# Encoder, window attention, encoder as one stream of 40 attention jobs, with the feed-forward inside the attention's steps

## The chip, the cores and the metric

The kernel runs on one core of a Trainium2 chip. A core has five engines that work at the same time, each through its own queue and in order: PE (matrix products), DVE (vector operations), ACT (activations and copies with a scale and a bias), POOL (GpSimd, here for selects, small vector work and gathers through lists of indices) and SP (which only starts transfers). They wait for each other by semaphores. PE's weight loads, PEld in the profile, overlap its products. PE writes to PSUM, eight banks of 128 partitions x 512 numbers. The metric is the time on the device in microseconds, the median of several runs.

## The reference

A network of 16 layers works on `x`, 8 batches of T = 256 tokens of D = 128 numbers (in some layers cut otherwise), each with a layer norm ahead and the result added to `x`. The change concerns the last three: a mixture of encoder layers, a banded attention, the same mixture again. Cut to these:

```python
x = x + L3_ffn(layernorm(x))          # encoder mixture
x = x + L3_attn_b(layernorm(x))       # banded attention, 16 heads of 8, window 64
x = x + L3_ffn(layernorm(x))          # encoder mixture again

def L3_ffn(x):                        # E = 4 experts, K = 2 are chosen per batch
    gate = x.mean(axis=1) @ gate_w.T + gate_b
    weights = softmax(gate) * (the two largest, per batch)
    return sum over experts of weights * encoder_layer(x, the expert's matrices)

def encoder_layer(x, ...):
    q, k, v = split(x @ iw.T + ib)                 # 16 heads of 8
    o = softmax(q @ k.T / sqrt(8)) @ v
    x = layernorm(x + o @ ow.T + ob) * n1w + n1b
    ff = relu(x @ l1w.T + l1b) @ l2w.T + l2b       # 128 -> 512 -> 128
    return layernorm(x + ff) * n2w + n2b
```

The kernel handles 8 batches of 256 tokens, so one encoder mixture is 8 x 2 = 16 jobs, each one batch through one expert.

## The kernel before

`Net.stages` lists the parts of the network, which run one after another. The last three are `encoder_moe` (L1999), `window` (which calls `attn8`, L1511) and `encoder_moe` again.

**An encoder stage.** First the layer norm of all 8 batches (`layernorm`, L1224): statistics of 16 tiles on DVE, a root on ACT and a reciprocal on DVE (`rstd_of`, L1189), then per batch the normalized rows `xn` and their transpose `xnT` over PE. Then the gate: mean over the tokens (`g_mean`), a product on PE (`g_ps`), and a chain of small DVE operations that finds the two experts of each batch, their weights (`g_wt`) and the rows at which the experts' matrices lie in HBM (`g_idx`). From here on each job's weights come by indirect gathers that POOL issues (L2076): `g_A` (774 numbers per partition, the matrices of q, k, v and the output projection), `g_RA` (256, biases), `g_B` (1024, the feed-forward's matrices) and `g_RC` (263, its biases and scales).

**The attention** of the 16 jobs is a pipeline over steps (`StripAttention`, run under a manual schedule: PE's order is the order of the code, while the other engines' orders are found by the scheduler of the framework). A job has four steps, one per group of four heads. In step s a *burst* (L117 to L150) computes the scores `ps_s` of group s (reduced by DVE to the negative row maxima `nsp`, L154) and, for group s-2, the scores once more, transposed and with the maximum subtracted, `ps_t`, of which ACT takes the exponential into `pt`. The maximum gets into the product through `ps_m` and `qa` (L183, L185). Behind the burst a step does what is entered for it: the product with the values `ps_o` for the group of step s-3 (`av`), then the parts of neighbouring jobs: q, k and v projections at -4, -2 and +1 steps from a job's start, the transposes and the division of the result (`half`, `ps_ot`), and two steps of `finish`: the transpose `ps_tr`, and the output projection `ps_r`, which DVE adds to `xr` (input and bias) and writes to `zt`. In this stage all eight PSUM banks are one ring, `sml`, of which each new product takes the next.

**The feed-forward** (`ExpertFeed`, L700) comes after the attention of all 16 jobs. Per job: `norm` (ACT writes `gxh`), `turn` (transposes `g_t`, ACT writes `gy` and `gyr` with the norm's scale and bias), `up` (`g_h`, two products of 2 x 256 columns; ACT and DVE write the rectified `g_hs`), `down` (`g_f`: identity times `gyr` plus four products, for each half of the tokens), then statistics, root, and the addition of the second norm's result to `x` (L790 to L805). The weights `g_B` of the first four jobs are gathered into `g_ring` during the attention's end; the other twelve go to tiles of their own (`g_late`), fetched as the feed-forward starts. PSUM is divided otherwise here: four banks `sml`, two for `g_t`, two for `g_f`.

**The window stage** (`attn8` with kind "w") is the same pipeline with 8 jobs, a band mask added to the scores, and selects on POOL that clear the weights outside the band (`keep01`, L1325). Its layer norm has statistics ahead for all batches, and rows and transposes per job inside the steps. Then the second encoder stage starts with its layer norm and its gate for all batches.

Of the kernel before, what the change touches and what calls it, by code (L numbers as in the profile page):

```python
# [40 lines left out]
class Job:  # L41
    def __init__(self, xT, w_q, w_k, w_v, b_q, b_k, b_v, finish):
        self.xT, self.w_q, self.w_k, self.w_v = xT, w_q, w_k, w_v
        self.b_q, self.b_k, self.b_v, self.finish = b_q, b_k, b_v, finish


class StripAttention:
# [19 lines left out]
    def __init__(self, net, wk, opens, scale, kind, ln):  # L67
        self.net, self.nc, self.wk, self.opens, self.ln = net, net.nc, wk, opens, ln
        self.scale, self.kind = scale, kind
        self.sb, self.tb = self.S_BLOCKS[kind], self.T_BLOCKS[kind]  # L70
        self.width = {None: 512, "c": 384, "w": 320}[kind]
        self.jobs = {}
# [30 lines left out]
    def burst(self, s, last):  # L103
        net, nc = self.net, self.nc
        halves = ((0, 1), (2, 3))
        tops, sums = {}, {}
        if 0 <= s < last:
            tops = {g: net.sml("ps_s") for g in (range(4) if self.kind else ())}
            for ps in tops.values():
                nc.tensor.matmul(  # L110
                    out=ps[:, : self.width], lhsT=net.identb,
                    rhs=net.masks[self.kind][:, : self.width], start=True, stop=False,
                )
        t = s - self.LAG
        if 0 <= t < last:
            jt, it = self.jobs[t // 4], t % 4
            jt.pts[it] = self.wk.tile(  # L117
                [P, 4, self.width], F32, tag="pt", name="pt", bufs=2 if self.kind is None else 4
            )
        for sub in range(2):  # L120
            calls, then = [[], []], []
            if 0 <= s < last:
                j, i = self.jobs[s // 4], s % 4
                for g in halves[sub]:
                    then.append(self.score(j, s // 4 % 2, i, g, tops.get(g), calls))
            if 0 <= t < last:
                for g in halves[1 - sub]:
                    then.append(self.weigh(jt, it, g, calls))
            for cs in calls:
                for c in cs:  # L130
                    nc.tensor.matmul(**c)  # L131
            for f in then:
                f()
        if 0 <= t < last and self.kind is not None:
            net.keep01(jt.pts[it], self.kind)

    def score(self, j, n, i, g, ps, calls):
# [4 lines left out]
        for c, (qt, k0, nk, c0) in enumerate(self.sb):  # L142
# [3 lines left out]
                    rhs=j.kT[r, i // 3, k0 : k0 + nk], start=self.kind is None,  # L146
                    stop=self.kind is None or c == 1,
# [4 lines left out]
        def top():  # L152
            if self.kind is None:
# [3 lines left out]
            else:  # L157
                for qt, k0, nk, c0 in self.sb:
# [6 lines left out]
    def weigh(self, j, i, g, calls):  # L165
# [3 lines left out]
        for c, (kt, q0, nq, c0) in enumerate(self.tb):  # L169
# [6 lines left out]
        out = j.pts[i][:, g, :]  # L176
        return lambda: nc.scalar.activation(out, ps[:, : self.width], AF.Exp, scale=self.scale)  # L177
# [10 lines left out]
    def av(self, n, i):  # L188
# [4 lines left out]
        net.av8(po, j.pts[i], j.va, 4 * i, self.O_BLOCKS[self.kind])  # L193
        nc.scalar.copy(j.oT[:, i, :], po[:, :T])  # L194

    def half(self, n, qt):
        net, j = self.net, self.jobs[n]
        if qt == 0:
            j.o = self.wk.tile([P, 2, D], F32, tag="o8", name="o8")
            j.end = j.finish(self.wk, j.o)  # L200
        net.normal8_half(self.wk, j.o, j.oT, qt)

    def open(self, n):
        j = self.jobs[n] = self.opens[n]()
        j.qa, j.pts = {}, {}

    def finish(self, n):
        f = next(self.jobs[n].end, None)
        if f:
            f()  # L210

    def run(self):
        ev = {}

        def at(s, order, f, *args):
            ev.setdefault(s, []).append((order, f, args))

        N = len(self.opens)
        av = self.AV[self.kind]
        for n in range(N):  # L220
            b = 4 * n
            for i in range(4):
                at(b + i, 9, self.lower, n, i)
                at(b + i + av, 1, self.av, n, i)
            at(b - 6, 0, self.open, n)
            if self.ln:
                at(b - 6, 0, self.net.ln_norm, n)
                at(b - 5, 5, self.net.ln_turn, n)
            for d, f in zip(self.QKV[self.kind], (self.q, self.k, self.v)):
                at(b + d, 3, f, n)  # L230
            e = b + av + 4
            at(e, 6, self.half, n, 0)
            at(e, 6, self.half, n, 1)
            at(e + 1, 4, self.finish, n)
            at(e + 2, 2, self.finish, n)
        for s in range(min(ev), max(ev) + 1):
            self.burst(s, 4 * N)
            for order, f, args in sorted(ev.get(s, ()), key=lambda e: e[0]):
                f(*args)
# [460 lines left out]

class ExpertFeed:
    JOBS = 2 * B

    def __init__(self, net, wk, zt, mv, wf, gather):
        self.net, self.nc, self.wk, self.zt, self.mv, self.wf = net, net.nc, wk, zt, mv, wf
        self.gather_rows = gather
        self.ring = net.w16.tile([P, 4, 1024], F32, tag="w16", name="g_ring")
        self.hs = net.w16.tile([P, 4, 4, T], F32, tag="w16", name="g_hs")
# [5 lines left out]
    def fetch(self, i):  # L714
        w = self.ring[:, i, :] if i < 4 else self.late.tile(
# [1680 lines left out]
```

## Time and profile before

| | us |
|---|---|
| median of 3 runs | 2954.19 (2953.16 to 2958.8) |
| the profiled execution | 2984.23 |
| its span, first to last instruction | 2982.5 |

| place in the span | us from its start |
|---|---|
| first encoder: attention's first step | 2011.6 |
| its last burst; first `g_h` of the feed-forward | 2305.9; 2320 |
| window stage in its steady steps | about 2437 to 2544 |
| second encoder: first step | 2582.6 |
| last `g_f` | 2977 |

The page of a profile lists, for each engine, busy time, its share and the number of instructions; then the span in 40 slices, a digit for the busy tenths of each (PEclk is the granted clock of PE in tenths); then groups of instructions by line and tile. A table of stretches gives, for each stretch of the span, its length and the busy time (and number of instructions) of PE, PEld, DVE, ACT and POOL, the mean clock, the mean busy share of the DMA engines and the GB/s that they moved. A row for a tile gives the least, median and longest duration in ns of each operation on it.

### The profile page before, as it was taken

Reading aid. Unit: us, or ns where it says so; the run is one execution under the profiler, and the core shown is the slowest. Engines: PE = TensorE matmul, PEld = TensorE weight load, DVE = VectorE, ACT = ScalarE, POOL = GpSimd, SP = SyncE. Lnnn points to the kernel's source line nnn. Section 1 sums busy time; section 2 is a strip of 40 time slices with the busy share of each in tenths; the row PEclk is TensorE's granted clock in tenths of the full one; section 3 lists DMA queues with packets and bytes.
Section 4 is the critical chain, followed back from the end, with each engine's and each line's share of the span. In section 5 each row is a group of like instructions: output and inputs, shape, how many; then the busy total and the mean of one; then the engine's idle time right before and its main releaser. Section 6 shows DMA issues by size and latency. Waiting matters only on the chain. (4 is left out here: it accounts for less than half of the span.)

```text
span 2982.5 us, 63419 instructions
## 1 busy us (share of the span) xinstructions
PE 2567.0 (86%) x25520; PEld 1823.8 (61%) x25520; DVE 1979.9 (66%) x5033; ACT 1466.6 (49%) x3385; POOL 1092.8 (37%) x1404
## 2 busy tenths in 40 slices
PE   5888779989599978875996699978999889699998
PEld 2444358866377756753665476645666667466667
DVE  3888856667566666545763677756777577577756
ACT  3666424455244433312651455535666545366654
POOL 3777559612398124122002444431110336311121
PEclk8999989999799989977998899988999899799999
DMA  3000000000000100012001200011110300111112
GB/s 101 0 1 1 31 29 1 1 2 2 2 1 1 57 1 2 1 54 20 2 19 46 11 1 1 1 29 54 32 30 13 107 2 3 39 53 30 29 61 68
DMA packets 41988, 70.03 MB, mean 23 GB/s; under 512 B 9048, under 2 KB 30560, under 8 KB 40928
## 3 DMA queue, kind: packets, MB, share of 16 engines
q0 software_dynamic: 12288, 42.17, 5.7%
q1 hardware_dynamic: 29408, 23.81, 2.7%
q8 instruction: 202, 3.31, 0.5%
q14 instruction: 90, 0.74, 0.1%
HBM read 58.88 MB, written 7.08 MB: 22 GB/s over the span
## 5 line engine op out<-in xcount | busy, mean ns | idle before, releaser
L177 ACT ACTIVATE pt<-ps_t 128x512 f32<-128x512 f32 (+2 forms) x896 | 430.9, 566 | 303.9 <-PE ps_t L131 294.7
L154 DVE TENSOR_REDUCE nsp<-ps_s 128x2 f32<-128x512 f32 x640 | 399.3, 684 | 96.4 <-PE ps_t L131 62.1
L131 PE MATMUL ps_t<-qa,k 32*128 32x256 f32 (+2 forms) x3584 | 443.3, 377 | 7.0 <-DVE qa L185 3.5
L131 PE MATMUL ps_s<-k,q 32*128 32x256 f32 (+2 forms) x3584 | 427.8, 380 | 5.8 <-ACT k L95 5.1
L131 PEld LDWEIGHTS ps_t<-qa,k 32*128 32x128 f32 x3584 | 327.8, 187 | 28.4 <-ACT q L83 10.9
L131 PEld LDWEIGHTS ps_s<-k,q 32*128 32x128 f32 x3584 | 296.1, 189 | 59.1 <-issue 35.6
L1290 PE MATMUL ps_o<-pt,vaug 128*32 128x256 f32 (+3 forms) x3840 | 226.3, 354 | 15.5 <-DVE nsp L154 3.7
L1330 POOL TENSOR_SCALAR_AFFINE_SELECT pt<-pt 128x768 f32<-128x768 f32 (+1 forms) x192 | 129.3, 705 | 224.8 <-ACT pt L177 176.4
L464 POOL TENSOR_TENSOR hw<-hw,hden 128x512 f32<-128x512 f32 x128 | 130.3, 1039 | 175.9 <-DVE hden L461 99.0
L984 POOL TENSOR_TENSOR h<-h,cs 128x512 f32<-128x512 f32 x128 | 166.1, 1317 | 61.3 <-DVE h L983 58.7
L1290 PEld LDWEIGHTS ps_o<-pt,vaug 128*32 128x32 f32 x3840 | 101.7, 109 | 115.1 <-DVE nsp L154 54.2
L159 DVE TENSOR_REDUCE nsp<-ps_s 128x1 f32<-128x128 f32 (+2 forms) x512 | 132.4, 330 | 54.7 <-PE ps_t L131 47.4
L558 POOL TENSOR_SCALAR oh<-iota,f_tr 128x128 f32<-128x128 f32 (+1 forms) x256 | 139.1, 552 | 78.5 <-PE f_xg L569 43.3
L2076 POOL DMA_INDIRECT g_A<-in_g_A,g_idx x32 | 30.4, 948 | 368.7 <-ACT oT L194 229.3
L1219 PE MATMUL ln_ps<-ident,xn 128*128 128x128 f32 x256 | 62.8, 352 | 112.9 <-DVE xn L1211 108.6
L185 DVE TENSOR_TENSOR qa<-q,ps_m 128x256 f32<-128x256 f32 x224 | 93.1, 415 | 91.8 <-PE ps_m L183 62.0
L995 PE MATMUL m_py<-h,ident 128*128 128x512 f32 x256 | 137.5, 645 | 18.2 <-POOL h L984 16.5
L983 DVE TENSOR_TENSOR_SCAN h<-m_da,db 128x512 f32<-128x512 f32 x128 | 150.2, 1206 | 3.4 <-POOL m_ug L901 1.4
L1219 PEld LDWEIGHTS ln_ps<-ident,xn 128*128 128x128 f32 x256 | 37.4, 162 | 140.6 <-issue 83.8
L183 PE MATMUL ps_m<-ident,nsp 128*128 128x128 f32 x448 | 96.5, 294 | 26.4 <-DVE nsp L154 18.8
L457 ACT ACTIVATE hw<-h_s,hm 128x256 f32<-128x256 f32 x256 | 117.3, 476 | 1.4 <-DVE hm L451 1.3
L977 ACT ACTIVATE m_da<-delta,m_a 128x510 f32<-128x510 f32 x128 | 87.3, 689 | 55.2 <-DVE h L983 52.9
(490 smaller groups left out, 6088.3 us busy)
## 6 DMA issues: line engine op xcount, KB each, us to landing
mw<-in_e_w SPq DMA_DIRECT2D x2, 2048.0 KB, 8.2
moe_x<-e_bx SPq DMA_DIRECT2D x4, 640.0 KB, 5.5
e_bx<-moe_x SPq DMA_DIRECT2D x4, 640.0 KB, 5.4
x<-in_x SPq DMA_DIRECT2D x4, 256.0 KB, 3.7
fraw<-in_f_wq SPq DMA_DIRECT2D x1, 1024.0 KB
fraw<-in_f_wk SPq DMA_DIRECT2D x1, 1024.0 KB, 11.1
w_f_wv<-in_f_wv SPq DMA_DIRECT2D x1, 1024.0 KB, 4.7
w_f_wout<-in_f_wout SPq DMA_DIRECT2D x1, 1024.0 KB, 6.8
```

The source lines that it names most:

```text
L131: nc.tensor.matmul(**c)
L154: nc.vector.tensor_reduce(col, ps.rearrange("p (q k) -> p q k", q=2), AX.X, ALU.max, negate=True)
L159: nc.vector.tensor_reduce(col[:, qt : qt + 1], ps[:, c0 : c0 + nk], AX.X, ALU.max, negate=True)
L177: return lambda: nc.scalar.activation(out, ps[:, : self.width], AF.Exp, scale=self.scale)
L457: nc.scalar.activation(w[:, c], ps[:, c // 2, (c % 2) * T : (c % 2 + 1) * T], AF.Exp, bias=m[:, c : c + 1], accum_out=den[:, c : c + 1],)
L464: nc.gpsimd.tensor_tensor(w[:, sl], w[:, sl], den[:, sl].unsqueeze(2).to_broadcast([P, 2, T]), ALU.mult)
L558: pool.tensor_scalar(oh[:, t, lo : lo + n], net.iota[:, 0:n], slot, None, ALU.is_equal)
L983: nc.vector.tensor_tensor_scan(h, da, db, 0.0, ALU.mult, ALU.add)
L984: nc.gpsimd.tensor_tensor(h, h, cs, ALU.mult)
L995: nc.tensor.matmul(out=self.py[k], lhsT=self.net.ident, rhs=h, start=n == 0, stop=n == 15)
L1290: self.nc.tensor.matmul(out=po[32 * i : 32 * i + 32, q0 : q0 + nq], lhsT=va[:, kt, h0 + i, :], rhs=pt[:, i, c0 : c0 + nq], start=n == 0, s ...
L1330: nc.gpsimd.affine_select(out=v, in_=v, pattern=[[0, 4], [step, n]], compare_op=ALU.is_ge, fill=0.0, base=base, channel_multiplier=cm,)
```

## The change

The three stages become one, `chain`. It puts 40 jobs into one `StripAttention`: 16 encoder jobs, 8 window jobs, 16 encoder jobs, 160 steps. Scores and weights of the job kinds follow one another in the bursts without a break.

- The **feed-forward** of an encoder job is a set of hooks of its own, counted from the job's start: fetch of `g_B` and `g_RC` at +6, `norm` at +10, `turn` at +11, the two products of `up` at +12 and +13, the two of `down` at +14 and +15. It so lies inside the steps of the three jobs behind. `g_B` goes to a ring of four for all jobs. The tile `g_f` is split by halves of the tokens, so that each `down` has a bank; all PSUM is one ring of eight.
- **Layer norms**: the first one stays as it was; those ahead of the window jobs and of the second encoder are made per batch (`ln_batch`), at steps 57 + 4b and 76 + 4b, the transposes one or two steps later. The **second gate** is computed for batches 0 to 1, 2 to 4 and 5 to 7, at steps 82/83, 94/95 and 106/107.
- The **roots** inside the stream (`g_rs`, `g_rs2`, `lb_r`) are no longer a root on ACT and a reciprocal on DVE but on POOL: an addition of eps and `pow` with -1/2, each on 128 x 2 numbers. The product of `g_rs2` with the gate's weight and the two operations for `g_nm` go to POOL too.
- The second norm's centring and scaling (`g_tt`) is done per half, straight from the bank; the last step (`x`) follows when the root is there.
- The weights `pt` are four buffers (two tiles of the large pool, two halves each) for all kinds; there were two for the encoder and four for the window.
- `attn8` stays for two other layers and is written on the same class, in the same order of PE.

```diff
+    def add(self, job):
+        n, av = len(self.jobs), self.AV[job.kind]
+        self.jobs.append(job)
+        b = 4 * n
+        for i in range(4):
+            self.at(b + i, 9, self.lower, n, i)
+            self.at(b + i + av, 1, self.av, n, i)
+        self.at(b - 6, 0, lambda: job.fill(*job.open()))
+        for d, f in zip(self.QKV[job.kind], (self.q, self.k, self.v)):
+            self.at(b + d, 3, f, n)
+        self.at(b + av + 4, 6, self.half, n, 0)
+        self.at(b + av + 4, 6, self.half, n, 1)
+        for d, order, f in job.hooks:
+            self.at(b + d, order, lambda f=f: f(job))
...
     def fetch(self, i):
-        w = self.ring[:, i, :] if i < 4 else self.late.tile(
-            [P, 1024], F32, tag=f"g_late{i}", name=f"g_late{i}"
-        )
+        w = self.ring[:, i % 4, :]
         self.gather_rows(None, "g_B", i, out=w)
...
+    def roots(self, mv, name, wi=None):
+        nc = self.nc
+        r = self.tile([P, 2], name, 3)
+        nc.gpsimd.tensor_scalar(r, mv[:, :, 1], EPS, None, ALU.add)
+        nc.gpsimd.tensor_tensor(r, r, self.net.mhalf, ALU.pow)
+        return r
...
+    def add(self, i, xr, r):
+        d = self.st[i]
+        z = d["z"] = self.tile([P, 2, D], "g_z", 3)
+        self.nc.vector.tensor_tensor(z, xr, r, ALU.add)
+        mv = self.stats(z)
+        d["rs"] = self.roots(mv, "g_rs")
+        d["nm"] = self.tile([P, 2], "g_nm", 3)
+        self.nc.gpsimd.tensor_tensor(d["nm"], mv[:, :, 0], d["rs"], ALU.mult)
+        self.nc.gpsimd.tensor_scalar(d["nm"], d["nm"], -1.0, None, ALU.mult)
...
+    def down(self, i, u):
+        net, nc, d = self.net, self.nc, self.st[i]
+        ps = net.sml("g_f")
+        sl = slice(u * P, (u + 1) * P)
+        nc.tensor.matmul(
+            out=ps[:, :D], lhsT=d["yr"][:, sl], rhs=net.ident, start=True, stop=False
+        )
+        for j in range(4):
             nc.tensor.matmul(
...
+        nc.vector.bn_stats(out=d["st"][:, u, :], in_=ps[:, :D])
+        nc.vector.bn_aggr(out=mv[:, u, :], in_=d["st"][:, u, :])
+        nc.vector.scalar_tensor_tensor(
+            t[:, u, :], ps[:, :D], mv[:, u, 0:1], d["r"][:, 0:D], ALU.subtract, ALU.mult
+        )
+        if u == 0:
+            return
+        rs = self.roots(mv, "g_rs2")
         wi = self.wf[:, i : i + 1]
-        nc.vector.tensor_scalar(rs, rs, wi, None, ALU.mult)
+        nc.gpsimd.tensor_scalar(rs, rs, wi, None, ALU.mult)
...
+    def chain(self):
...
+            sa = StripAttention(self, wk, lambda t: pts[t % 2][:, t // 2 % 2])
+            for i in range(2 * B):
+                sa.add(self.encoder_job(wk, gates[0], ring, i))
+            for b in range(B):
+                n = len(sa.jobs)
+                sa.at(4 * n - 7, 0, self.ln_batch, b)
+                sa.at(4 * n - 5, 5, self.ln_turn, b)
+                sa.add(self.window_job(wk, b))
+                end = 4 * n + sa.AV["w"] + 7
+                sa.at(end, 0, self.ln_batch, b)
+                sa.at(end + 1, 5, self.ln_turn, b)
+                for b0, b1 in ((0, 2), (2, 5), (5, 8)):
+                    if b1 == b + 1:
+                        sa.at(end + 2, 0, gates[1].means, b0, b1)
+                        sa.at(end + 3, 5, gates[1].choose, b0, b1)
+            for i in range(2 * B):
+                sa.add(self.encoder_job(wk, gates[1], ring, i))
+            sa.run()
...
+        av = StripAttention.AV[None]
+        hooks = [(av + 5, 4, first), (av + 6, 2, second)]
+        for d, order, f, args in (
+            (av + 3, 0, feed.fetch, ()), (av + 7, 0, feed.norm, ()), (av + 8, 5, feed.turn, ()),
+            (av + 9, 7, feed.up, (0,)), (av + 10, 7, feed.up, (1,)),
+            (av + 11, 7, feed.down, (0,)), (av + 12, 7, feed.down, (1,)),
+        ):
+            hooks.append((d, order, lambda j, f=f, args=args: f(i, *args)))
```

## The prediction

> **What bounds the kernel now.** I read the page first, then a table of busy time for chosen stretches, then the durations of single tiles, and last PE's instructions in order.
>
> The page says where the change lies and that PE is nearest to full:
>
> ```profile
> span 2982.5 us, 63419 instructions
> PE 2567.0 (86%) x25520; PEld 1823.8 (61%) x25520; DVE 1979.9 (66%) x5033; ACT 1466.6 (49%) x3385; POOL 1092.8 (37%) x1404
> ...
> PE   5888779989599978875996699978999889699998
> ...
> PEclk8999989999799989977998899988999899799999
> ...
> q8 instruction: 202, 3.31, 0.5%
> ```
>
> A slice is 74.6 us. The code that is changed is the last third, slices 27 to 40, from about 1985 us. PE dips at 2535 to 2610, with a clock of 0.7: a seam between stages. The stretches show it closer (length; PE, PEld, DVE, ACT, POOL busy; clock; share of the DMA engines; GB/s):
>
> ```profile
> 1985.00:2012.00 27.00, 9.27 (x54) 5.18 (x58) 12.69 (x48) 5.73 (x13) 9.53 (x11) 0.54 0.27 78
> 2060.00:2074.00 14.00, 11.17 (x128) 6.86 (x127) 7.18 (x18) 5.82 (x12) 6.41 (x7) 0.88 0.57 189
> 2100.00:2150.00 50.00, 50.00 (x774) 34.44 (x766) 38.90 (x87) 33.03 (x72) 7.92 (x9) 1.00 0.13 34
> 2300.00:2350.00 50.00, 35.09 (x287) 24.45 (x283) 17.84 (x60) 24.00 (x56) 20.16 (x24) 0.80 0.39 125
> 2350.00:2400.00 50.00, 50.00 (x361) 46.98 (x360) 41.84 (x178) 31.21 (x78) 6.14 (x12) 1.00 0.11 35
> 2450.00:2500.00 50.00, 48.46 (x992) 37.96 (x989) 35.27 (x139) 29.90 (x85) 34.35 (x50) 1.00 0.01 3
> 2540.00:2583.00 43.00, 21.60 (x332) 13.91 (x328) 20.63 (x81) 14.14 (x34) 18.83 (x26) 0.70 0.18 50
> ```
>
> In mid-attention (2100), mid-feed-forward (2350) and the window stage (2450) PE is full: PE bounds each stage. In the seams (2300, 2540) it idles 15 and 21 us. DVE is the next engine, at 78% and 84%.
>
> **What the seams are worth.** PE's instructions in order give the steady durations. An encoder attention step is 4.2 to 4.75 us, a job of four 18.05; a feed-forward job is 4.18 (g_h 1.73, g_t 0.22, g_f 2.23); a window job is 16.5. Back to back: 32 x (18.05 + 4.18) + 8 x 16.5 = 843 us. From the first step (2011.6) to the end (2982.5) it takes 971. So 127 us are fill, drain, bursts of gathers and seams. The changed kernel still ends with one drain: last half, rowproj, norm, turn, up, down, which I estimate at 33 us (from the last burst at 2305.9 to the first g_h at 2319 it is 13 now, then one feed-forward job with nothing to cover its chain). At most 95 us can go.
>
> **A second, small gain.** Of the 18.05, about 1.06 is PE waiting for a bank: a burst is 1.94 us unhindered and 2.24 to 2.76 in the steps after q and k. With feed-forward matmuls between bursts, ACT has more time for q and k. The job in the new kernel is then 17.0 + 4.18 + some 0.1 for remaining waits = 21.3 us, for 22.23 now.
>
> **What it costs: the queue of GpSimd.** PE's order is written by hand, the others' by the scheduler; each engine works through its queue in order. Put in order for the changed kernel, POOL's queue per encoder job reads: g_ring gather of job i+4 (its buffer is free when PE ends job i's last down matmul, at T), rs2 add of job i, g_RC gather of job i+4, pow, times wi, gbb of job i+4 (waits for g_RC to land), g_A, xr, then g_rs. DVE's queue has the two x updates that need rs2 directly behind t, and behind them the reductions of the next burst. The rows for it:
>
> ```profile
> L2076 POOL DMA_INDIRECT g_ring<-in_g_B,g_idx x8: 937/943/962, 2062.1 to 2637.8; - x8
> ...
> L741 POOL TENSOR_TENSOR gbb<-g_RC x32: 192/200/460, 2016.2 to 2953.1; 128x1 f32<-128x1 f32 x32
> ...
> L1193 DVE RECIPROCAL g_rs<-g_rs x34: 152/155/353, 2317.8 to 2978.5; 128x2 f32<-128x2 f32 x32, 128x32 f32<-128x32 f32 x2
> ```
>
> A gather holds POOL 0.94 us, with some 0.30 before the next. So from T: gather 1.25, add to 1.5, gather to 2.7, pow and times wi to 3.3, two x updates on DVE (0.35 each) to 4.0, reduction of the first score bank (0.68) to 4.7. PE, after ps_m (0.31) and a burst (1.94), wants that bank for ps_o at T + 2.25. It waits about 2.5 us, once per job. Without the two gathers ahead the chain would end about when PE comes. In each half the 12 jobs that still have a fetch ahead of them pay it: 24 x 2.5 = 60 us. In the first half five ln_batch calls come between as well (lb_r stands behind gbb, xn on DVE waits for lb_r): 5 x 1.3 = 6.5.
>
> **pow has no row.** The trace has no GpSimd pow at all. Nearest is gbb, a GpSimd operation of the same size: 0.20, at most 0.46. From below it costs what gbb does (0 extra; a gain is excluded, since it stands beside gbb-sized operations already counted). From above I allow 1 us, the size of a gather's hold. I take 0.2 extra, gbb's longest. It counts on two chains per job, rs2 and the first norm (g_rs, g_nm, g_nm, gxh on ACT, and exps behind gxh): 24 x 2 x 0.2 = 10 us. The Trainium skill speaks against the move: GPSIMD Engine Reference, section 3.1, has elementwise work belong on DVE, with a two-input operation measured 1.96 times as long on GpSimd. By it each small operation would be 0.155 (the reciprocal's row) x 1.96 = 0.30, an estimate; against gbb's 0.20 that is 0.1 x 3 operations x 24 = 7 us, within what I have added. A second rule, SBUF — State Buffer, section "Who interferes with whom", is that a DVE instruction with two SBUF inputs holds off a GpSimd instruction that reads SBUF. gbb's spread of 0.19 to 0.46 allows it, and no row here proves it; in the merged steps DVE runs such x updates, which is why I take the longest and not the median. By the median the sum would be 10 us less.
>
> **Gathers beside PE.** At step 11 now, four 512 KB gathers (2062 to 2068, row 2060) make the step 9.35 us for 4.2; 2.8 us of it PE waits for nothing that the profile shows. PE's own instructions come by DMA too (queue q8), so code fetched late is a candidate, not shown. The steady stage, with g_A and g_RA per job, has 1.0 us of such idle in 50 us, 0.36 per job. With g_B and g_RC per job as well, I add the same again: 24 x 0.36 = 9. From below 0, from above the 2.8 of the burst for 32 jobs, 90.
>
> **The window part.** 8 x 16.5 = 132. Three feed-forward jobs of the first half fall in: 3 x 4.18 = 12.5. Eight turns of the second norm: 8 x 0.54 = 4.3 (two ln_ps of 0.27). POOL has 34.35 busy of 50 here (the select of the band), so lb_r comes late and DVE stands at xn: about 2.5 us in five of the eight = 12.5, an estimate from the same chain. Three gate chains of some 20 small DVE operations (0.16 to 0.23): 3 us each in front of reductions, 9. At steps 84 to 88, 16 gathers (16 x 1.25 = 20 us) stand in POOL's queue ahead of lb_r and the selects; POOL has 6.4 of 20 us free, so 13.6 are lost. Together 184. (Of these, the loads of the gathers would otherwise lie in the seam.)
>
> **The sum**, on the trace's clock. Step 10 at 2063 (2060.2 now; the four g_ring gathers come earlier, in the fill, and I give them 3 of the 5 us that they cost now). Steps 10 to 15, 6 x 21.3/4 = 32: 2095. Steps 16 to 63, 12 x 21.3 = 256, + 30 + 6.5: 2387.5. Window: 2571.5. Steps 96 to 105, without feed-forward, 10 x 4.51 = 45 and a burst as now at 2635 (6.9): 2623.5. Six more, 32: 2655.5. Steps 112 to 159, 255.6 + 30: 2941. Drain 33: 2974. pow 10, gathers 9: 2993. That is +10.5 us on the span of 2982.5; the profiled execution was 2984.23, 1% over the median of the runs, 2954.19, and I carry the difference over: **2965 us**. The removed Sqrt on ACT (0.29) and its reciprocal are worth nothing here; ACT is not the bound. The rewriting of the causal and dual attention leaves PE's order as it is: 0.
>
> **The rivals.** What differs under 0.2% (6 us) a measurement of this kernel can't tell from no change.
>
> *A, as summed: the queue of GpSimd gives the seams back.* Chance 0.42. For it: the order of the queues and the 0.95 gather. Its own range is 2935 to 2995, so it holds all three outcomes (0.13 faster, 0.07 same, 0.22 slower).
>
> *B, the wait is covered; the seams are gained.* The place is ps_o in the step after down, the price A's 2.5 us per job. If rs2's add, pow and product run before the gathers, or the scores' reductions before the x updates, ps_o finds its bank. Each 0.44 us less of wait per job is 10.5 us: below 2.06 us the kernel is faster. If all of it is covered, 60 + 10 + 9 fall away: 2914 on the trace's clock, 2886 by median; with the window's backlog covered too, 2860. For it: DVE has 20% to spare in a merged job (14.0 + 3.5 of 21.3 us). Against it: the updates stand right behind t, with nothing between. Chance 0.29, faster.
>
> *C, pow or the gathers are dear.* At pow = 1 us both chains grow by 0.8 where I have 0.2: + 24 x 2 x 0.6 = 29, giving 2994; with gathers at 2.8 us for each job it is + 81, 3046. Without the terms of pow and gathers A would end 8 us faster than now, and each 0.1 us of pow takes 5 us of it. Chance 0.20, slower.
>
> *D, DVE becomes the bound.* Its 17.5 busy plus waits for semaphores fill the job to 22.2: + 0.9 x 24 = 22, 2987. For it: 84% in the feed-forward. Against: sum of busy time is 82%. Chance 0.09, slower.
>
> That the change doesn't do what it says is excluded for the order, which is on PE by hand.
>
> **How the numbers follow.** Faster 0.13 + 0.29 = 0.42, same 0.07, slower 0.22 + 0.20 + 0.09 = 0.51. The range runs from 2880, which leaves out the lower half of B (about 0.12), to 3035, above which a third of C lies (0.07).
>
> **What would show it.** Right: in each encoder job one PE wait of 2 to 3 us before ps_o released by DVE nsp, in the step after down; DVE idle before x released by POOL rs2; POOL idle before g_ring released by PE g_f. The seam at 2540 gone, clock at 1.0 there. Encoder job near 24 us with those waits. Wrong, towards B: a job of 21.3 us and a last feed-forward near 2900. Wrong, towards C: pow rows of 0.6 us or more, or PE idle without a releaser of over 1 us per job. Wrong at the window: steps 84 to 88 without a wait for POOL pt.

## The result, and the profile after

The changed kernel takes 3072.03 us (median of 4 runs, 3067.35 to 3075.9) for 2954.78 (4 runs): a ratio of 1.0394, interval 1.0376 to 1.0412. It is 3.9% slower, 107 us above the forecast and above its range. The profiled execution took 3071.11 us.

From the page, in the order of the page before:

```profile
span 3069.0 us, 63959 instructions
PE 2586.8 (84%) x25524; PEld 1842.6 (60%) x25524; DVE 1985.4 (65%) x5018; ACT 1454.6 (47%) x3346; POOL 1199.2 (39%) x1660
...
PE   5888689989599887957976999978888987888887
...
PEclk7999889999799998978988999989999998999999
...
L1380 PE MATMUL ps_o<-g_pt,vaug 128*32 128x256 f32 (+2 forms) x2816 | 167.0, 362 | 99.8 <-DVE nsp L161 82.4
```

The deep dips of the old seams are gone, but where PE had 9 for most of a stage it now has 8 nearly everywhere. The last row says where: PE stood 99.8 us ahead of `ps_o`, 82.4 of it until DVE had written `nsp`.

One job of the second encoder, by its four steps, from the table of stretches (the first two rows are one step, cut at the end of the wait; columns as before: length; PE, PEld, DVE, ACT, POOL busy; clock; DMA share; GB/s):

```profile
2819.30:2824.50 5.20, 2.17 (x33) 1.72 (x32) 2.20 (x8) 2.06 (x4) 3.32 (x5) 1.00 0.40 127
2824.50:2829.40 4.90, 4.88 (x40) 2.96 (x40) 2.98 (x6) 2.33 (x6) 0.19 (x1) 0.65 0.00 0
2829.50:2834.60 5.10, 5.10 (x87) 3.92 (x86) 4.65 (x12) 2.64 (x7) 1.25 (x2) 1.00 0.02 3
2834.70:2840.80 6.10, 5.37 (x77) 3.90 (x76) 3.33 (x7) 3.17 (x8) 2.87 (x6) 1.00 0.34 86
2840.90:2846.50 5.60, 5.60 (x71) 4.55 (x70) 4.48 (x13) 4.18 (x10) 0.00 (x0) 1.00 0.01 3
```

In the step after the last down matmul PE works 2.17 of 5.20 us. Then comes a row in which PE is busy throughout and the clock is 0.65: what follows the wait (`ps_o`, q, `ps_tr`, `g_h`, `ps_m`) takes 4.95 us, where the same instructions take 3.32 in the jobs in which the clock stayed. The fourth row, the step with k and the first down of the next job, has another 0.73 us of idle PE. The steps are 10.2, 5.2, 6.2 and 5.7 us long, 27.3 together; with no wait and the full clock, the same instructions are 5.26, 5.10, 5.34 and 5.51, or 21.2.

The waits of PE between 2700 and 3032 us (total, times, longest):

```profile
PE ps_o L1380 <- DVE nsp L161: 36.7, 12, 3.1
PE g_f L863 <- ACT g_pt L184: 7.2, 9, 1.3
```

The first is the forecast wait, once per job. The second is the 0.73 us of the fourth row. What feeds both is on POOL, in the rows of the root's tile:

```profile
L798 POOL TENSOR_SCALAR g_rs<-g_mv x64: 217/221/262, 2061.6 to 3059.7; 128x2 f32<-128x2 f32 x64
L799 POOL TENSOR_TENSOR g_rs<-g_rs,mhalf x64: 707/732/756, 2063.1 to 3060.0; 128x2 f32<-128x2 f32 x64
L884 POOL TENSOR_SCALAR g_rs<-g_rs,g_wt x32: 298/298/303, 2099.3 to 3060.8; 128x2 f32<-128x2 f32 x32
...
  DVE x L890: 80.5, 32
```

`pow` takes 0.73 us, and DVE's updates of `x` waited 80.5 us for these operations. Two rows for the other terms, the gather and `gbb`:

```profile
L774 POOL DMA_INDIRECT g_ring<-in_g_B,g_idx x32: 934/1070/1092, 2026.3 to 3007.4; - x32
```

```profile
L829 POOL TENSOR_TENSOR gbb<-g_RC x32: 183/193/498, 2012.0 to 3013.2; 128x1 f32<-128x1 f32 x32
```

Put in order of time for that job, T = 2819.14 being the end of the last `g_f`: statistics, aggregate and `g_tt` on DVE to T+1.1; on POOL the `g_ring` gather 2819.41 to 2820.50, the addition at 2820.57, the `g_RC` gather 2821.07 to 2822.05, pow 2822.08 to 2822.81, the product with the weight 2822.92 to 2823.22; the first `x` on DVE at 2823.25, after 2.97 us of idle DVE; the first reduction at 2823.78. PE gets its bank at 2824.52, after 3.06 us in one piece.

**Where the 117 us are.** The 24 steady jobs (steps 16 to 63 and 112 to 159) take 327.9 + 321.9 = 649.8 us. The same 24 jobs cost 24 x 22.1 = 530 before: 4.18 of feed-forward and 17.92 of attention, the mean of two kinds of job of 17.8 and 18.05 us, of which the prediction took the longer. These 119 us are the whole loss. Everything else from the first step to the end is 409 us after and 413 before (on a chip of the same kind, see the last experiments): nearly all that the seams gave back, the window part took.

### The profile page after: what moved, and what is told of

Its sections match the earlier page's. It is cut to its first block, busy times and chain, and to the rows that moved or that the text cites. A ratio compares the mean times of both kernels' runs of the same rounds, so it can differ in the third digit from the quotient of the medians.

```text
span 3069.0 us, 63959 instructions
## 1 busy us (share of the span) xinstructions
PE 2586.8 (84%) x25524; PEld 1842.6 (60%) x25524; DVE 1985.4 (65%) x5018; ACT 1454.6 (47%) x3346; POOL 1199.2 (39%) x1660
## 5 line engine op out<-in xcount | busy, mean ns | idle before, releaser
L184 ACT ACTIVATE g_pt<-ps_t 128x512 f32<-128x512 f32 (+1 forms) x640 | 311.1, 568 | 197.4 <-PE ps_t L137 189.8
L137 PEld LDWEIGHTS ps_t<-qa,k 32*128 32x128 f32 x3584 | 336.5, 188 | 20.6 <-ACT q L89 4.4
L137 PEld LDWEIGHTS ps_s<-k,q 32*128 32x128 f32 x3584 | 304.4, 190 | 54.6 <-issue 31.4
L1380 PE MATMUL ps_o<-g_pt,vaug 128*32 128x256 f32 (+2 forms) x2816 | 167.0, 362 | 99.8 <-DVE nsp L161 82.4
L1380 PEld LDWEIGHTS ps_o<-g_pt,vaug 128*32 128x32 f32 x2816 | 75.1, 113 | 173.8 <-DVE nsp L161 115.9
L184 ACT ACTIVATE pt<-ps_t 128x384 f32<-128x384 f32 (+1 forms) x256 | 118.9, 552 | 87.0 <-PE ps_t L137 86.3
L201 ACT COPY oT<-ps_o 128x256 f32<-128x256 f32 x224 | 86.2, 386 | 108.6 <-PE ps_o L1380 108.4
L774 POOL DMA_INDIRECT g_ring<-in_g_B,g_idx x32 | 33.5, 1046 | 218.4 <-PE ps_m L190 216.2
```

The source lines that it names most:

```text
L184: return lambda: nc.scalar.activation(out, ps[:, :width], AF.Exp, scale=j.scale)
L774: self.nc.gpsimd.indirect_dma_start(out=out, out_offset=None, in_=src, in_offset=bass.IndirectOffsetOnAxis(ap=self.idx[:, which, i : i + 1 ...
L1380: self.nc.tensor.matmul(out=po[32 * i : 32 * i + 32, q0 : q0 + nq], lhsT=va[:, kt, h0 + i, :], rhs=pt[:, i, c0 : c0 + nq], start=n == 0, s ...
```

## The experiments

Chips differ: the kernel before takes 2952 to 2956 us on most of those used here, 2982 to 2988 on two. Each was used only once, so what is called the chip here can be anything else that was the same for all runs of that time. Ratios to the kernel before on the same chip are compared. "Step" means PE's time from one burst to the next. A job's four, means of the 11 jobs of steps 112 to 155, are given in this order: the step after the last down matmul (with q and the first up), the next one (second up), the one with k and the first down, the one with the last down.

| run | ratio, interval | the four steps, us |
|---|---|---|
| changed kernel | 1.0394 (1.0376 to 1.0412) | 10.04, 5.27, 6.01, 5.70 |
| e1 cheap root | 1.0221 (1.0198 to 1.0243) | 8.77, 5.56, 5.55, 5.70 |
| e2 POOL in code order | 1.0424 (1.0401 to 1.0447) | 7.50, 5.80, 7.36, 6.34 |
| e3 DVE in code order, `x` late | 1.0316 (1.0292 to 1.0340) | 5.54, 7.39, 6.89, 5.84 |
| e4 both | 1.0192 (1.0169 to 1.0215) | 5.55, 7.53, 5.71, 5.81 |
| e11 few gathers | 1.0198 (1.0181 to 1.0215) | 7.18, 5.77, 6.02, 5.69 |
| e5 `x` two steps later | 1.0405 (1.0387 to 1.0422)* | 5.55, 6.12, 5.71, 10.66 |
| e6 and g_hs shared otherwise | 1.0312 (1.0293 to 1.0331)* | 5.55, 5.41, 5.34, 10.63 |
| e7 and ln_batch in two parts | 1.0229 (1.0202 to 1.0255)* | 5.55, 5.41, 5.34, 10.63 |
| e15, e7 again | 0.9987 (0.9978 to 0.9995) | 5.54, 5.42, 5.33, 6.85 |
| e8 and the fetch earlier | 0.9986 (0.9979 to 0.9994) | 5.55, 5.41, 5.34, 6.85 |
| e10 and `x` in three steps | 0.9909 (0.9893 to 0.9926) | 5.55, 5.41, 5.33, 6.07 |
| e12, e10 with four gathers in a row | 0.9912 (0.9896 to 0.9929)* | 5.55, 6.31, 5.69, 6.07 |
| e18, e12 again | 0.9943 (0.9927 to 0.9960) | 5.55, 5.41, 5.53, 6.07 |

\* on a chip where the kernel before takes 2982 us (e5 to e7) or 2988 (e12).

**e1: is it pow?** The sum of the wait's chain says that pow's 0.73 us sits on it twice per job. The edit turns it into a product with zero, at both places, so the roots are left out:

```diff
-        nc.gpsimd.tensor_tensor(r, r, self.net.mhalf, ALU.pow)
+        nc.gpsimd.tensor_tensor(r, r, self.net.mhalf, ALU.mult)
...
-        nc.vector.memset(self.mhalf, -0.5)
+        nc.vector.memset(self.mhalf, 0.0)
```

> Left out: the roots of the stream; pow is replaced by a product with zero, so the normalized rows are zeros and only the biases reach x. Each root is 0.2 us instead of 0.73. Theory 1 (POOL's queue holds DVE's x update, and PE's wait of 3.1 us behind it is long enough that its clock falls to half for the next products, 1.6 us per job): the wait falls to 2.5 us, the clock stays at 1.0 in most jobs, the encoder job goes from 27.3 to about 24.6 us, the kernel to about 3005 us. Theory 2 (the same queue, but the slow products have another cause): 0.53 us on each of two chains, 24 jobs, so 26.3 us per job and about 3045. Theory 3 (gathers that delay PE's code, or DVE as the bound): within 5 us of 3072.

Measured: 3020.56 us, between the two. The row of the same tile and line:

```profile
L799 POOL TENSOR_TENSOR g_rs<-g_rs,mhalf x64: 194/207/218, 2060.8 to 3006.8; 128x2 f32<-128x2 f32 x64
```

The product takes 0.21. The wait in the burst shrinks by 0.5 us, from 3.3 to 2.8, the k step by 0.46, and the window (steps 64 to 96) from 192.5 to 181.1 us. The step after down falls by 1.27, though, more than the wait: the clock fell behind the wait in 13 of 24 jobs, for 20 of 24 in the changed kernel (in one more of each it fell for a part). pow is worth 51 us (1.0394 less 1.0221, of 2954; the slow clock that it brings is in it), and most of the loss is not pow.

**e2: the order on POOL.** The two gathers stand ahead of pow since the scheduler orders POOL's queue. Here it keeps the order of the code, as PE's does.

```diff
-            es.enter_context(self.tc.manual_schedule(engines={mybir.EngineType.PE}))
+            es.enter_context(self.tc.manual_schedule(engines={mybir.EngineType.PE, mybir.EngineType.Pool}))
```

> POOL in the order of the code, as PE: roots ahead of the gathers, nothing else changed. Theory 1: rs2 is there 1.75 us earlier, PE waits 1.3 us before ps_o in the step after down, no clock drop, and the 0.8 us in the step of k go (no g_RA gather between g_rs and pow): job 23.1 us, kernel about 2970. Theory 2: job 24.7, about 3010. Theory 3: 3072, since the gathers are the same and as many.

Measured: 3080.67 us, no gain. The step after down fell from 10.0 to 7.5, but DVE's queue, still ordered by the scheduler, holds an update of `x` with the bias of job i+4 (L886) that waits for its `g_RC`, which now is fetched late; it stood there 4.3 to 5.3 us in every second job, and the reductions behind it. One of them:

```profile
DVE x L886 <- DMA g_RC<-in_g_RC,g_idx: 5.2, 1, 5.2
```

**e3, e4: the updates of x behind the next burst.** Nothing needs `x` so early. In e3 DVE follows the code, and the updates are entered in the next step; in e4 POOL follows the code too.

```diff
-            es.enter_context(self.tc.manual_schedule(engines={mybir.EngineType.PE}))
+            es.enter_context(self.tc.manual_schedule(
+                engines={mybir.EngineType.PE, mybir.EngineType.DVE}
+            ))
...
+            (av + 13, 8, feed.close, ()),
```

> DVE in the order of the code, and the two x updates that need rs2 (with the bias update) moved from the step of the last down to behind the next burst; POOL is left to the scheduler, gathers ahead of roots. Theory 1: rs2 comes as late as before, but no reduction stands behind it; the wait of 3.1 us and the slow products go, the 0.8 us in the step of k stay: job 22.4 us, kernel about 2955. Theory 3 (DVE bound or gathers): no more than 10 us from 3072.

> Both: POOL and DVE in the order of the code, and the x updates behind the next burst. Theory 1: job 21.6 us, near the 21.0 of PE's own work; 24 jobs x 5.7 us less, about 2930, faster than the kernel before, whose seams it no longer has. Theory 3: within 10 us of 3072.

Measured: 3050.96 and 3011.73. The step after down is 5.54, as expected: no wait there, and no fall of the clock. But the wait moved on by one step. DVE's waits in e3, 2710 to 3016:

```profile
DVE g_st L875 <- PE g_f L867: 41.6, 25, 4.9
DVE g_hs L855 <- ACT g_hs L857: 29.3, 24, 3.1
```

`g_hs` is rectified by DVE and ACT in turns; DVE waits for ACT's half, which stands behind q, and the updates of `x` then come ahead of the reductions. The step after that is 7.4 for 5.2. Removing one wait of an in-order queue exposed the next.

**e11: the gathers alone.** The changed kernel, with the gathers of the feed-forward's weights left out for 12 of 16 jobs of each half.

```diff
-        self.gather_rows(None, "g_B", i, out=w)
-        self.st[i] = dict(w=w, r=self.gather_rows(self.wk, "g_RC", i, 4))
+        if i < 4:
+            self.gather_rows(None, "g_B", i, out=w)
+            self.kept = getattr(self, "kept", []) + [self.gather_rows(self.wk, "g_RC", i, 4)]
+        self.st[i] = dict(w=w, r=self.kept[i % 4])
```

> The changed kernel with one thing left out: from the fifth job of each half on, g_B and g_RC are not gathered and the first four jobs' weights are used again (12 of 16 jobs compute with wrong experts' feed-forward weights). The roots stay on POOL, DVE's order stays with the scheduler. Theory 1: the chain behind the last down loses the 2.3 us of two gathers and their gaps, PE waits about 1.3 us for 3.1, its clock stays, the job goes from 27.3 to about 24.0 us, the kernel to about 2990. If the roots alone (pow 0.73) made the wait: no more than 15 us less than 3072.

Measured: 3012.9. The wait is 2.0 us, not gone:

```profile
PE ps_o L1382 <- DVE nsp L161: 16.3, 11, 1.8
```

With POOL free at T, statistics, aggregate, addition, pow and product (0.3, 0.17, 0.22, 0.71, 0.30 and the hand-overs) end at T+2.3. In half of the jobs three updates of `x`, 1.1 us, then stand ahead of the first reduction, at T+3.35; in the changed kernel it is two in every job. In the six jobs of the second encoder in which it is two here as well, the wait is 1.5 us (1.25 in one piece). So of the 3.3 us the gathers made 1.3 to 1.8 and the chain itself 1.5 to 2.0. The clock fell in 3 of 24 jobs only.

**e5, e6, e7: the next waits, one by one.** e5 is e4 with the updates at +15; e6 gives both halves of the first product to DVE and both of the second to ACT; e7 runs `ln_batch` in two parts a step apart, so that POOL has time for `lb_r`.

```diff
-            (av + 13, 8, feed.close, ()),
+            (av + 15, 8, feed.close, ()),
...
-            if j % 2:
+            if not a:
...
-                sa.at(4 * n - 7, 0, self.ln_batch, b)
+                sa.at(4 * n - 8, 4, self.ln_batch, b)
+                sa.at(4 * n - 7, 4, self.ln_rows, b)
```

> As e4, with the bias and the two x updates moved by two steps more, to the step of the first down of the next job. What is left in e4 is a wait of 2.3 us in the burst of the step after up: DVE's reductions stand behind g_hs (which waits for ACT, that has q before it) and behind the three x updates (1.2 us). Theory: the updates' part goes, g_hs's stays: 1.0 to 1.2 us per job, 24 jobs, about 2985 us. If the x updates were not what delays the reductions: 3010 as e4.

> As e5, and up's rectification is divided otherwise: both halves of the first product on DVE, both of the second on ACT (before: one of each on each), so that DVE does not wait for ACT in the step in which ACT evacuates q. Theory: the burst is 1.94 to 2.2 us in all four steps, the job 21.9 us, about 2950 us in all. Rival: DVE's load in that step (0.48 us more) makes its reductions as late as ACT's did: 2985.

> As e6, and the layer norms per batch are cut in two: statistics and root in one step, the rows xn in the next (DVE no longer stands at xn while POOL has its selects ahead of lb_r). Theory: the window's steps 64 to 95 take about 175 us for 200 in e4, so 25 less than e6, about 2925. Rival: the window's waits come from the gathers and the gate chains: within 5 us of e6.

Measured: 3103.98, 3074.2 and 3046.45. The waits aimed at are gone (the first three steps are 5.55, 5.41, 5.34), and e7 takes 22 us from the window (200 to 178). But the fourth step went from 5.8 to 10.6. From e7's table of stretches:

```profile
2242.00:2244.00 2.00, 2.00 (x23) 1.33 (x21) 0.00 (x0) 0.01 (x1) 1.58 (x2) 1.00 0.77 230
2244.00:2246.00 2.00, 0.96 (x4) 0.55 (x4) 1.14 (x4) 1.75 (x4) 0.00 (x0) 1.00 0.56 209
2246.00:2248.00 2.00, 1.32 (x12) 0.72 (x11) 1.97 (x6) 0.17 (x1) 0.00 (x0) 1.00 0.02 6
2248.00:2251.00 3.00, 3.00 (x25) 1.92 (x24) 1.46 (x3) 2.23 (x5) 0.00 (x0) 0.63 0.00 0
```

Four gathers land (DMA share 0.77), then PE runs only 16 matmuls in 4 us, and the clock falls to 0.63. I took this for PE standing with no wait in the records, and the four gathers in a row for the cause.

**e8, e9: the gathers apart.** The fetch of `g_B` and `g_RC` goes two steps ahead, in e7's kernel (e8) and in e4's (e9).

```diff
-            (av + 3, 0, feed.fetch, ()), (av + 7, 0, feed.norm, ()), (av + 8, 5, feed.turn, ()),
+            (av + 1, 8, feed.fetch, ()), (av + 7, 0, feed.norm, ()), (av + 8, 5, feed.turn, ()),
```

> As e7, with the fetch of g_B and g_RC two steps earlier: two gathers in one step and two in another, where e7 (as e4, e5, e6) issues all four in the step of the first down. In e7 PE stands 2 to 3 us in that step in each job with gathers, with no wait in the records, and its clock falls behind it. Theory (four gathers in a row, 1.2 MB in 5 us, are what holds PE): the wait goes, job 22.1 us for 26.5, about 4% less than e7. Rival (DVE's updates of x in that step): as e7.

> As e4, with the fetch moved as in e8. In e4 the step with four gathers shows no wait, and the wait of 2.3 us in the step behind up does not depend on gathers: within 10 us of e4 (ratio to the kernel before 1.016 to 1.022). If gathers do cost e4 time, it is faster by more.

Measured: 2948.74 us (ratio 0.9986) with the fourth step at 6.85, and 3011.08 (1.0190, interval 1.0169 to 1.0210), as e4. That looked like the proof, but e8 ran on another chip than e7.

**e13 to e16: the chip or the gathers?** Both kernels and e7's and e8's, unedited, on one chip.

> The kernel before, profiled on the chip that this call is given. Its profiled execution so far took 2984.23 us, its timed runs have medians of 2952 to 2956 on three chips and 2982 and 2988 on two. If the 30 us are a property of the chip (theory K), this run's profile agrees with its own median within 0.3%, at about 2954 or at about 2984, whichever kind of chip it is. If the first 2011 us of the span do not move (first steps of all kernels so far lie at 2005 to 2015 on both kinds of chip), a 30 us shorter span has them all in the last third: in the two seams, where the clock was 0.54 to 0.80, or at the bursts of gathers. If instead profiling itself cost this kernel 1% (rival), the profile is at 2984 and the median at 2954 again.

> The changed kernel on the same chip. Its ratio to the kernel before was 1.0394. Theory K, the chip shifts both alike: ratio 1.039 again, a profile of about 3071 on a chip of the 2954 kind, of about 3100 on one of the 2984 kind. Rival, the chip's kind moves only the kernel before: 3071 in both, and the ratio on a chip of the 2984 kind is 1.029. Step after down 10.0 us in either.

> The kernel in which PE stood in the step of the four gathers in a row (step of the second down 10.63 us, ratio 1.0229, on a chip where the kernel before takes 2982). If the place of the gathers does that, the step is 10.6 here whatever the chip. If the chip did it, then on a chip of the 2954 kind the step is about 6.9, as in the kernel with the gathers spread, and the ratio near 0.999.

> The same with the fetch two steps earlier (step of the second down 6.85 us, ratio 0.9986, on a chip where the kernel before takes 2952). If the place of the gathers matters, 6.85 here too, and the two kernels differ by 2.4%. If the chip, then on a chip of the 2984 kind the step is near 10.6; on one of the 2954 kind the two kernels of this call are alike.

Measured: 2954.74, 3074.09 (1.0394), 2949.71 (0.9987) and 2950.61 (0.9981). The stall isn't there in e15 either: 6.85. So my explanation of e5 to e7 falls: the chip made the stall, and the earlier fetch is worth 0.06% here, within the intervals. (e8's kernel was not run on a chip with the stall.) The same kernel on the two chips, e7 and then e15, in the rows of ACT over the first encoder's steady jobs (2100 to 2400 and 2100 to 2360), shows that it isn't PE that stands first:

```profile
L101 ACT ACTIVATE k<-ps_k,g_A 128x256 f32<-128x256 f32 x22 | 9.2, 470 | 22.2 <-PE ps_t L137 16.4 <-issue 4.3 <-PE ps_m L190 1.5
L101 ACT ACTIVATE k<-ps_k,g_A 128x256 f32<-128x256 f32 x20 | 8.7, 509 | 0.0
```

In e7 ACT stood 1.4 to 2.9 us ahead of k in 20 of the 24 steady jobs; in e15 never. In the job of the table above `ps_k` was written by 2241.0, and k began at 2243.99. Between 2100 and 2400 PE's recorded waits include 8.8 us for this k and 2.4 for DVE's `g_tt`, which came late as well; e15 has neither.

The profile of the kernel before on this chip (span 2951.8) shows the same thing at the place that the prediction read as a burst of gathers:

```profile
2060.00:2074.00 14.00, 14.00 (x209) 9.53 (x203) 10.51 (x23) 9.85 (x22) 5.97 (x7) 1.00 0.61 190
```

The same stretch in the prediction had 11.17 busy of 14.00 and a clock of 0.88, at the same GB/s. Step 11, 9.35 us there, is 4.18 here; there, too, ACT had stood ahead of its k (3.2 us, at 2067.8), here it did not. The 30.7 us between the two spans are 3.1 in the first attention, 8.2 in the first feed-forward, 3.3 in the window stage, 4.5 and 8.9 in the second encoder, 2.7 ahead of all. What it is in such a chip that holds ACT and then PE while gathers land is open.

**e10, e17: a version that beats both.** e8 with the three updates of `x` in three steps, so that no reduction waits for more than one of them.

```diff
+            (av + 13, 0, feed.bias, ()),
+            (av + 15, 8, feed.close, (0,)), (av + 17, 0, feed.close, (1,)),
```

> As e8, with the three updates of x taken apart: the bias update one step behind the last down, the first half of the tokens two steps later, the second half two steps after that. In e8 the step behind the first down still has a burst of 3.28 us for 2.23 in a job without updates ahead of its reductions. Theory (what stands before the reductions in DVE's queue is what PE pays, instruction by instruction): 0.8 us per job, 24 jobs, 19 us: about 2930, ratio to the kernel before 0.992. Rival (the two gathers left in that step cause it): as e8.

> The kernel with the x updates in three steps and the fetch two steps earlier: job 22.47 us, ratio 0.9909 on a chip where the kernel before takes 2953. On a chip of that kind the same again. On one of the other kind (kernel before near 2984, PE idle without a wait at bursts of gathers): if spreading the gathers avoids that idle, 2928 again and a ratio of 0.981; if not, 0.991.

Measured: 2928.05 us (0.9909) and, on another chip, 2928.4 (0.9917, interval 0.9900 to 0.9933): 0.9% faster than the kernel before. Its steps 16 to 63, and under it the same stretch of the changed kernel:

```profile
2083.40:2353.10 269.70, 269.70 (x3654) 199.21 (x3654) 212.87 (x511) 179.73 (x391) 89.20 (x156) 1.00 0.17 51
```

```profile
2095.60:2423.50 327.90, 282.76 (x3653) 205.84 (x3653) 213.29 (x529) 177.85 (x391) 91.11 (x160) 0.94 0.14 41
```

The work is the same, 12 jobs. PE is busy all of 269.7 us at the full clock, where it was busy 283 of 328 at 0.94. A job is 22.5 us for 27.3. Of the 1.3 us above the 21.2, 1.2 are in three of the four bursts, which take 2.23, 2.26 and 2.49 us where the fourth takes 1.94: small waits, which this view counts as busy.

**e12, e18: four gathers in a row.** e10 with the gathers `g_A` and `g_RA` moved to where `g_B` and `g_RC` are.

```diff
-        self.at(b - 6, 0, lambda: job.fill(*job.open()))
+        self.at(b - 8, 9, lambda: job.fill(*job.open()))
```

> As e10, but g_A and g_RA are gathered in the same step as g_B and g_RC again, now in the step behind the last down: four gathers in a row as in e5 to e7, at another place, with the updates of x where e10 has them. If four in a row are what holds PE: a wait of 2 to 3 us once per job and a slower clock behind it, job about 26 us for 22.4, about 3020 us. If it was their place in e7 (the step of k and the first down), or something else there: within 10 us of e10.

> The same with the four gathers of a job in a row, in the step behind the last down: job 23.86 us and ratio 0.9912 on a chip where the kernel before takes 2988. If the row of gathers costs the 1.3 us per job, whatever the chip, the ratio is 0.991 + 24 x 1.3 / 2953 = 1.001 on a chip of the 2953 kind. If the chip cost it, the job is 22.5 there and the ratio 0.991 again.

Measured: 2963.5 us (0.9912) with a job of 23.6 us where the kernel before takes 2988; on the usual kind of chip 2935.69 us (0.9943) with a job of 22.6, beside e17's 0.9917 and 22.4 on that chip. So 1.0 of the 1.2 us per job was the chip's. What is left for the row is 0.26% or some 7 us by the medians, and the intervals overlap.

## Why the prediction was wrong

The mechanism and its place were right; several sizes were not, the largest missing term was not in the sum, and the step from the trace to the median was wrong. The sum gave 24.6 us per steady job: 21.3 without waits, 2.5 of wait, 0.4 for pow, 0.4 for gathers. Measured is 27.3 in a job in which the clock fell: 21.2, 3.3, 1.6 for the clock, 0.8 in the k step, 0.4 of small waits in the other bursts. The mean of the 24 jobs is 27.1.

- **"It waits about 2.5 us, once per job"**: right in place, releaser and number of times. It measured 3.3. e1 splits it: 2.8 with a product of 0.21 us in the place of pow, 0.5 more from pow.
- **"Without the two gathers ahead the chain would end about when PE comes"**: wrong. I began the chain with the gathers at T and left out the 0.8 us of statistics, which the first gather hid, and had addition, pow and product at 0.85 us where e11 shows 1.4. e11 measured a wait of 2.0 us without the gathers, 1.5 where nothing else had slipped in. The rival in which the wait is covered was too likely for that reason.
- **"pow has no row"**: the step that chose the value. "I take 0.2 extra, gbb's longest" was some 0.3 us short per chain; the row says 0.73, three and a half times the product on the same tile (0.21). The upper bound of 1 us held it. A row of the same size says little where the operation differs: the 0.30 that I estimated for any small operation is above the addition (0.22) and the product (0.21) and far under pow. In the norm's chain PE waited 0.8 where I had 0.2; e1 took 0.46 of it away.
- **The clock: not in the sum.** The first table that I showed had 0.54 and 0.70 in the stretches where PE idles, and I priced the idle alone. Once PE had stood 3.06 us, the next 4.9 us ran at 0.65: q, `ps_tr` and `g_h` took 1.44, 0.48 and 1.71 for 0.98, 0.27 and 0.87. It is 1.6 us each time: with the same wait the step is 8.55 where the clock stayed, 10.2 where it fell. After waits of 3.3 us the clock fell in 20 of 24 jobs, after 2.8 in 13 (e1), after 2.0 in 3 (e11). Two waits of the changed kernel, with the fall and without it, show what seems to decide:

```profile
2822.44:2825.85 3.41, 1.33 (x26) 0.81 (x29) 2.60 (x7) 0.40 (x2) 0.86 (x3) 1.00 0.28 88
2825.85:2829.27 3.42, 3.42 (x20) 2.15 (x12) 1.63 (x4) 2.02 (x5) 0.00 (x0) 0.50 0.00 0
2955.56:2958.97 3.41, 1.63 (x28) 1.21 (x20) 0.42 (x3) 2.06 (x4) 2.90 (x5) 1.00 0.49 157
2958.97:2962.39 3.42, 2.15 (x35) 1.22 (x36) 3.01 (x6) 0.52 (x2) 0.19 (x1) 1.00 0.25 74
```

  In this profile every spell of the half clock from step 10 on starts on one grid of 3.41 us, whose steps these rows are, and those of the steady jobs last one step (one lasts two). The step ahead of a spell had PE idle for 1.93 us or more; up to 1.78 us of idle no spell followed, and once at 2.05 none did. (In e11 three spells followed 1.76 to 1.83 us, so idle time alone gives no sharp limit.) The wait of 3.06 us leaves 2.08 us of it in one step of the grid in the first pair, at most 1.78 in the second. And a job with the fall lasts 27.3 us, eight steps of the grid, so that the next wait lies at the same place: from step 112 on nine jobs in a row fell. This is read from the traces; no run moved a wait along the grid without changing it. The Trainium skill, TensorE: Matmul & The Clock Gate, "What's actually happening", has the clock halved after an idle window of about 3.4 us, with windows that run freely. The length and the free run agree with the grid; but 3.06 us in one piece, or 1.8 in e11, is shorter than such a window, so to wait for a gap of 3.4 us before counting the cost would have missed all of it. Over the 24 jobs it is 34 us, nearly half of the 76 that the sum lacked.
- **"Gathers beside PE ... 9"**: nothing; e10 has all these gathers and PE busy throughout. The 1.0 us of idle that I read in the steady stage is that of the weight loads, which overlap; PE itself was busy 50.00 of 50.00 there. The upper bound came from the burst at step 11, which is the chip's. The third rival's 3046 lay nearest to the result, for a cause that isn't in it.
- **"I carry the difference over"**: 28 us too low. I took the 1% between the profiled execution (2984) and the median (2954) for a factor. It is the difference between two kinds of chip: e13 profiles the same kernel at 2953.59. The sum had removed most of these places by pricing the new stream without them, and then I subtracted the same 30 us again. The profile of the changed kernel stands at its own median.
- **The window, 184**: 192.5; e1 and e7 say what was short: pow in `lb_r` (11) and the row of `ln_batch` in one step (e7 takes 22 from the 200 of e6). Steps 96 to 105 took 57.5 for 52, the next six 36.5 for 32, steps 10 to 15 35.75 for 32, the drain 37 for 33.
- **"At most 95 us can go"**: some 67 on the chips that the median is from, since 28 of the 127 us were the chip's (30.7 less the 2.7 ahead of the first step), and 4 less by the drain, which takes 37. Nothing of it was in reach while each job lost 5 us; e10 got 26.
- **The rule on shared SBUF** between DVE and GpSimd: pow (0.707 to 0.756) and the addition (0.217 to 0.262) hardly vary, so nothing of it shows in them. The longest `gbb`, 0.498 for a median of 0.193, is not explained.
- **Rival D**, DVE as the bound: not so. In the steady steps DVE is busy 213 of 328 us, 65%; what counted was the order in its queue.

The account: 3069.0 less the sum's 2993 is 76. Steady jobs 52.7 (71.7 measured above their estimate, less the 19 of pow and gathers that the sum held apart); window 8.5; the steps around it 13.75; drain 4; an earlier start of step 10 takes 3. The other 31 of the 107 is the carry-over.

## What to carry to other kernels

When small operations move to an in-order queue, price the whole chain from the last producer to the next consumer, statistics included, and enter the operation's own time, by measurement, not that of another one of the same size. A wait of PE of 2 to 3 us can cost more than its length: here up to 1.6 us of slow clock came behind it, and more often the longer it was and the more of it lay in one step of the grid. And move what nobody needs yet (here the update of `x`) behind the work that is waited for, step by step, looking each time at which wait comes next: all of the loss and a gain of 0.9% lay in the order and the division of such small work.

## What was not expected of the hardware

- pow on GpSimd takes 0.73 us on 128 x 2 numbers, a product 0.21, an addition 0.22.
- The half clock comes in spells on a grid of 3.41 us, behind a step of the grid in which PE idled for some 1.8 to 2 us or more: behind the same wait it costs 1.6 us or nothing, it seems by where the wait lies.
- Chips differ by 1% for this kernel, and by more for others: e7's kernel has a ratio of 1.0229 on one and 0.9987 on another, nearly all of it in one step of 10.6 or 6.85 us. While gathers land, ACT stands 1.4 to 2.9 us ahead of an operation whose input is there, and PE runs out of banks behind it; why is open. No run of the changed kernel fell on such a chip.
